# The last projection of a graph network, in seven block products for pairs of row blocks

## The chip, the cores and the metric

The kernel runs on one core of a Trainium2 chip. The metric is the device time of one execution in microseconds. Engines are named as in the profile: PE is TensorE (PEld its weight loads), DVE is VectorE, ACT is ScalarE, POOL is GpSimd, SP is SyncE, which only issues transfers here.

## The reference

Everything is float32: x is [1024, 512], there are 16384 edges, 16 blocks of conditioning [256, 512], and four layers of attention and gated feed-forward between two graph convolutions.

```python
def _gcn(x, src, dst, W, b, n):
    deg = segment_sum(ones_like(src), dst, n)
    dinv = where(deg > 0, deg ** -0.5, 0)
    norm = dinv[src] * dinv[dst]
    h = x @ W
    return segment_sum(h[src] * norm[:, None], dst, n) + b

h0 = relu(layernorm(x))
h = batchnorm(h0);  h = _gcn(h, ..., gcn_in_w, gcn_in_b, n)
for i in range(4):
    h = h + attention(ln(h), cond, Wq[i], Wk[i], Wv[i], Wo[i])
    val, gate = split(ln(h) @ geglu_w[i] + geglu_b[i])
    h = h + (val * gelu(gate)) @ ffo_w[i] + ffo_b[i]
h = _gcn(h, ..., gcn_out_w, gcn_out_b, n)
out = x + h + h0
```

The change is about `x @ W` of the last `_gcn`: [1024, 512] times [512, 512].

## The kernel before, in words

The 1024 rows are eight row blocks of 128 (NB = 8), kept in SBUF as `h[0]` to `h[7]`. A 128x128 block of the edge-count matrix for each pair of row blocks is `counts[d][:, s, :]`; the graph convolution is then a matrix product (`aggregate`, L648 to L659). It takes the projected rows in two parts, high and low (`parts_out`), that are each exact in the twelve-bit format of its matmuls.

Most large products are computed with seven block products instead of eight: a matrix is split into 2 x 2 blocks, sums of blocks are made beforehand (`sums_of_a` and `sums_of_b`, four additions or subtractions each), and the seven products are put together in PSUM and by additions. `multiply` (L301) issues one block product, two matmuls over the two halves of a 256-long sum. `attn_out_pair` (L852 to L883) is an earlier use on two row blocks with two PSUM banks, ab and cd, each of which holds two 256-wide results. `wo_sums` makes the four sums of a weight matrix on GpSimd into the one tile `wos`.

The last stage, before the change:

- In the last layer's last part (r = 3), `load_last` fetches the last weight `w_out` (two transfers on SP's queue) and its bias, and issues the reload of the counts (`ce`) on GpSimd's queue. Also in the last two parts, `base_of` makes `base` = x + h0 for each row block on VectorE.
- `ffn_out` finishes h in two steps, s = 0 (row blocks 0, 1, 4, 5) and s = 1 (2, 3, 6, 7).
- `turn_first` turns the eight row blocks on TensorE (L184) and copies them out of PSUM into `lnT` (tile name ln2T), two copies each on ScalarE (L1106).
- L1315 and L1316: GpSimd adds the bias to the eight `base` tiles.
- `project_block` (L461) computes one row block of the projection with four matmuls of a 512-wide moving tile; `into_parts` scales it into the high part on ScalarE (L1321) and takes the low part on VectorE (L1322).
- L1332: a branch that is taken only when the edges are not sorted by destination; here it is not. L637 has the same one ahead of the first aggregation.
- `aggregate` (L655), and `into_out` (L1327, L1328) per row block: VectorE scales and adds `base`, SP stores.

The order in which instructions stand on each engine's queue is set before the run by the framework's planner: it takes the instructions in the order in which the code traces them as their priority, simulates the engines, and lets a later one go first where an earlier one is not ready in its simulation. A branch splits the program into stretches that are planned one by one. `tc.issue_after` and `waiting_for` force an order by hand; none is used in the last stage. Tiles come from pools of a fixed number of buffers: `psum` eight banks, `work` ten tiles of 128x512 (`t512`), `accs` six of them (`acc_tile`), `slots` 36 of 128x1024.

Of the kernel before, what the change touches and what calls it, by code (L numbers as in the profile page):

```python
# [14 lines left out]
OP = mybir.AluOpType  # L15
AX = mybir.AxisListType

P = 128
# [5 lines left out]
def gnn_kernel(  # L24
# [26 lines left out]
    nc = tc.nc  # L51
# [3 lines left out]
    BS, M, DC = cond.shape  # L55
# [4 lines left out]
    NB = N // P  # L60
# [31 lines left out]
    def bank(name):  # L92
        return psum.tile([P, 512], F32, tag="bank", name=name)

    def t512(name, dtype=F32):
        return work.tile([P, 512], dtype, tag="t512", name=name)
# [4 lines left out]
    def slots_of(n, name):  # L101
        return [slot(f"{name}_{i}") for i in range(n)]

    def load_w(w2d, name):

        w = slots_of(2, name)
        for i in range(2):
            load_w.last = nc.sync.dma_start(
                w[i], w2d[2 * i * P:2 * (i + 1) * P, :].rearrange("(k p) f -> p k f", p=P)
            )  # L110
        return w

    def load_row(vec, offset, name):
        t = rows.tile([P, D], F32, tag="row", name=name)
        nc.sync.dma_start(
            t, bass.AP(tensor=vec.tensor, offset=vec.offset + offset, ap=[[0, P], [1, D]])
        )
        return t

    def four(t):  # L120
        return t.rearrange("p (a b) -> p a b", a=4)
# [58 lines left out]
    def transposed(t, name):  # L180

        pt = bank(f"tr_{name}")
        for k in range(4):
            transposed.last = nc.tensor.transpose(pt[:, k * P:(k + 1) * P],  # L184
                                                  t[:, k * P:(k + 1) * P], ident)
        return pt
# [30 lines left out]
    def sums_of_a(t, a11, a12, a21, a22, s1, s2, s4):  # L217

        t.tensor_tensor(s1, a21, a22, OP.add)
        t.tensor_tensor(a21, a11, a21, OP.subtract)  # L220
        t.tensor_tensor(s2, s1, a11, OP.subtract)
        t.tensor_tensor(s4, a12, s2, OP.subtract)

    def halves_of(t):
        return t.rearrange("p (a b) -> p a b", a=2)
# [70 lines left out]
    def multiply(to, left, right, cols_of, start):  # L296

        for n, (l0, l1, r0, r1) in enumerate(cols_of):
            at = to if len(cols_of) == 1 else to[:, n * (r1 - r0):(n + 1) * (r1 - r0)]
            for k in range(2):  # L300
                nc.tensor.matmul(at, left[:, k, l0:l1], right[:, k, r0:r1],  # L301
                                 start=start and n == 0 and k == 0,
                                 stop=n == len(cols_of) - 1 and k == 1, skip_group_check=True)
# [67 lines left out]
    first = gp.tile([P, 2], F32, name="first")  # L371
# [53 lines left out]
    for nb, xn in enumerate(scaled(xb, mean, root, "x", xb)):  # L425
        with tc.issue_after(cond_turned.ins):
            pt = transposed(xn, f"x{nb}")
        c0 = (nb % 4) * P
# [38 lines left out]
    def project_block(*args):  # L467
        for _ in project_steps(*args):
            pass
# [175 lines left out]
    def of_twelve_bits(rows):  # L645
        return [t.bitcast(F32R) for t in rows]

    def aggregate(parts, name, emit):  # L648

        for ds in [(0, 1), *((d,) for d in range(2, NB))]:  # L650
            pa = [bank(f"agg_{name}_{d}") for d in ds]
            for s in range(NB):
                for d, to in zip(ds, pa):
                    for i, part in enumerate(parts):
                        nc.tensor.matmul(to, counts[d][:, s, :], part[s],  # L655
                                         start=(s == 0 and i == 0),
                                         stop=(s == NB - 1 and i == 1))
            for d, to in zip(ds, pa):
                emit(d, to)  # L659

# [21 lines left out]
    def acc_tile(name):  # L682
        return accs.tile([P, 512], F32, tag="acc", name=name)
# [148 lines left out]
    def wo_sums(wo):  # L832

        b11, b12, b21, b22 = (wo[k][:, :, d * M:(d + 1) * M] for k in range(2) for d in range(2))
        t1, t2, t3, t4 = (halves_of(wos[:, i, :]) for i in range(4))
        for to, of, less in ((t1, b12, b11), (t3, b22, b12), (t2, b22, t1), (t4, b21, t2)):
            nc.gpsimd.tensor_tensor(to, of, less, OP.subtract)
        return [b11, b21, b22, t4, t1, t2, t3]
# [46 lines left out]
    def order7(blk, s1, s2, s4):  # L885

        return [blk[0], blk[1], s4, blk[3], s1, s2, blk[2]]
# [20 lines left out]
    class Quad:  # L908
# [3 lines left out]
        def __init__(self, l, r, c, left, right, fT):  # L912
            self.n, self.c, self.fT = f"{l}_{r}_{c}", c, fT
            self.cv = l * 2 * DFF // P + r * KC + c
            self.left, self.right = left, right

        def product(self, i, to, start):
            multiply(to, self.left[i], self.right[i],
                     [(self.c * P, (self.c + 1) * P, 0, 512)], start)

        def first(self):
            self.a = bank(f"ga_{self.n}")
            self.product(0, self.a, True)
            self.s1 = acc_tile(f"gs1_{self.n}")
            nc.scalar.copy(self.s1, self.a)
# [8 lines left out]
        def rest(self):  # L934
            n, c, bias = self.n, self.c, gcols[:, self.cv:self.cv + 1]
            pb, pc, pd = (bank(f"{x}_{n}") for x in ("gb", "gc", "gd"))
            self.product(5, pb, True)
            u2 = acc_tile(f"gu2_{n}")
            nc.vector.tensor_tensor(u2, pb, self.s1, OP.add)
            self.product(6, pc, True)  # L940
            u3 = acc_tile(f"gu3_{n}")
            nc.vector.tensor_tensor(u3, pc, u2, OP.add)  # L942
            self.product(4, pd, True)
            g1 = t512(f"g1_{n}")
            nc.vector.tensor_tensor(g1, pd, u3, OP.add)  # L945
            self.gate(g1, n)
            self.product(3, pc, False)
            g0 = t512(f"g0_{n}")
            nc.vector.tensor_tensor(g0, pc, u2, OP.add)
            self.gate(g0, n)  # L950
            self.product(2, pd, False)
            v1 = acc_tile(f"gv1_{n}")
            nc.vector.scalar_tensor_tensor(v1, pd, bias, u2, OP.add, OP.add)
            f0, f1 = (self.fT[i][c // 2][:, c % 2, :] for i in range(2))
            nc.vector.tensor_tensor(f1, v1, g1, OP.mult)
            return lambda: nc.vector.scalar_tensor_tensor(f0, self.a, bias, g0, OP.add, OP.mult)
# [140 lines left out]
    def turn_first(l, blocks):  # L1097

        for nb in blocks:
            xn, c0 = xns.pop(nb), nb % 4 * P  # L1100
            if l < L:
                turn(xn, lnT[nb // 4], c0, LN2W + l * KC, LN2B + l * KC, f"ln2_{l}_{nb}")
            else:
                pt = transposed(xn, f"hT_{nb}")
                for k in range(2):
                    nc.scalar.copy(lnT[nb // 4][k][:, :, c0:c0 + P],  # L1106
                                   four(pt)[:, 2 * k:2 * k + 2, :])

    lnT = [slots_of(2, f"ln2T_0_{i}") for i in range(2)]
    aggregate(parts_in, "in", into_h_and_norm)  # L1110
# [12 lines left out]
        return (wk, wv, *load_rest(l))  # L1123

    def load_last():
        w = load_w(gcn_out_w, "w_out")
        bias = load_row(gcn_out_b, 0, "bias_out")
        again = slots_of(NB, "ce")
        for d in range(NB):
            counts[d] = by_sources(again[d].bitcast(F32R))  # L1130
            nc.gpsimd.dma_start(again[d].bitcast(F32R).rearrange("p a b -> p (a b)"), c_dram[d])
        return w, bias
# [8 lines left out]
    for l in range(L):  # L1141
# [40 lines left out]
        right = [ln3T[0][0], ln3T[0][1], ln3T[1][1], ln3S[2], ln3S[0], ln3S[1], ln3T[1][0]]  # L1182
# [73 lines left out]
        lnT = None  # L1256
        base, fetched = [], {}
# [14 lines left out]
        for r in range(R):  # L1272
# [27 lines left out]
            else:  # L1300
                lnT = [slots_of(2, f"ln2T_{l + 1}_{i}") for i in range(2)]
                if last:
                    w_out, bias_out = load_last()
# [8 lines left out]
    ready_first(L, left_to_turn[2:])  # L1312
    turn_first(L, left_to_turn)

    for nb in range(NB):  # L1315
        nc.gpsimd.tensor_tensor(base[nb], base[nb], bias_out, OP.add)  # L1316
    hs_out = [rows_of("hs_high_out"), rows_of("hs_low_out")]
    parts_out = [of_twelve_bits(rows) for rows in hs_out]

    def into_parts(nb, ph):  # L1320
        nc.scalar.mul(parts_out[0][nb], ph, dinv[:, nb:nb + 1])  # L1321
        nc.vector.scalar_tensor_tensor(parts_out[1][nb], ph, dinv[:, nb:nb + 1],  # L1322
                                       hs_out[0][nb], OP.mult, OP.subtract)

    def into_out(d, pa):
        ot = t512(f"ot_{d}")
        nc.vector.scalar_tensor_tensor(ot, pa, dinv[:, d:d + 1], base[d], OP.mult, OP.add)  # L1327
        nc.sync.dma_start(out[d * P:(d + 1) * P, :], ot)  # L1328

    for nb in range(NB):  # L1330
        project_block(nb, lnT, w_out, "out", into_parts)
    with tc.If(unsorted > 0):  # L1332
        add_left(slot("left_out"), hs_out, base, dinv, "out")
    aggregate(parts_out, "out", into_out)


# [35 lines left out]
```

## Time and profile before

| | us |
|---|---|
| median of 3 runs | 2534.37 (2533.81 to 2534.73) |
| the profiled execution | 2532.89 |
| its span in the profile | 2531.1 |
| PE busy | 2506.6 (99%) |
| DVE busy | 1403.6 (55%) |
| POOL busy | 646.0 (26%) |
| ACT busy | 557.3 (22%) |
| granted TensorE clock, mean | 1.0 |

Matmul durations overlap, since matmuls are pipelined: the pace is read from the starts of consecutive ones. Each f32 matmul appears as two instructions ("passes" below). A timeline row gives start, duration, engine, line, operation, out<-in tiles and shapes, and in brackets how long the engine had been idle and what released it. A summary of a tile gives minimum/median/maximum duration in ns and the first and last start in us.

### The profile page before, as it was taken

How to read it: one execution, taken by the hardware profiler on the slowest of the kernel's cores; microseconds unless marked ns; L12 is line 12 of the kernel's file. 1: busy time of each engine (PE TensorE's matmuls, PEld its weight loads, DVE VectorE, ACT ScalarE, POOL GpSimd, SP SyncE). 2: the span in 40 equal slices, each digit the busy share in tenths (PEclk: the TensorE clock that was granted, in tenths of full speed). 3: DMA queues.
4: the chain of work that ended last, by engine and by line, in shares of the span. 5: the costliest groups of instructions: out<-in, count | busy, mean ns of one | idle time of the engine just before them, and what ended most of it. 6: DMA issues, size and time to landing. Idle time of an engine off the chain costs nothing. (4 is left out here: it accounts for less than half of the span.)

```text
span 2531.1 us, 32228 instructions
## 1 busy us (share of the span) xinstructions
PE 2506.6 (99%) x12464; PEld 1768.6 (70%) x12464; DVE 1403.6 (55%) x3026; ACT 557.3 (22%) x1318; POOL 646.0 (26%) x539
## 2 busy tenths in 40 slices
PE   8999999999999999999999999999999999999999
PEld 5778886666578887655587888556676888566565
DVE  9655566544574556544474556644484455654551
ACT  7322222111122223111122222111112222211111
POOL 0322224532210003533320003253320002352410
PEclk9999999999999999999999999999999999999999
DMA  5302232111122112010211212110112121111020
GB/s 179 131 31 91 92 128 64 38 50 35 61 64 70 46 59 76 26 54 17 96 38 67 72 63 67 34 55 17 59 67 64 53 78 60 44 34 64 11 88 34
DMA packets 67136, 156.81 MB, mean 62 GB/s; under 512 B 5576, under 2 KB 5904, under 8 KB 66976
## 3 DMA queue, kind: packets, MB, share of 16 engines
q1 hardware_dynamic: 64880, 149.25, 17.8%
q0 software_dynamic: 1376, 4.30, 0.5%
q8 instruction: 103, 1.69, 0.3%
q10 hardware_dynamic: 720, 1.11, 0.1%
q14 instruction: 57, 0.47, 0.1%
HBM read 133.66 MB, written 20.97 MB: 61 GB/s over the span
## 5 line engine op out<-in xcount | busy, mean ns | idle before, releaser
L301 PE MATMUL ga<-ln3T,wval 128*128 128x512 f32 x512 | 233.9, 593 | 0.0
L932 ACT ACTIVATE g<-g,gcols 128x512 f32<-128x512 f32 x128 | 92.4, 722 | 430.9 <-DVE g L945 366.3
L301 PEld LDWEIGHTS ga<-ln3T,wval 128*128 128x128 f32 x512 | 96.0, 190 | 109.9 <-issue 109.0
L776 ACT ACTIVATE pr<-sc,nmax 128x256 f32<-128x256 f32 x256 | 118.0, 473 | 176.8 <-DVE nmax L771 176.8
L847 POOL TENSOR_TENSOR os<-oT 128x256 f32<-128x256 f32 x12 | 8.7, 726 | 566.9 <-DVE oT L822 566.9
L1006 POOL TENSOR_TENSOR hall<-fu,hall 128x512 f32<-128x512 f32 x24 | 30.4, 1269 | 429.0 <-DVE fu L1005 429.0
L301 PE MATMUL pa_v<-wv,ct 128*128 128x256 f32 x512 | 123.1, 379 | 0.0
L301 PE MATMUL fa<-wff,fT 128*128 128x256 f32 x512 | 121.6, 379 | 0.0
L301 PE MATMUL gc<-ln3S,wgate 128*128 128x512 f32 x256 | 120.4, 593 | 1.1 <-DVE gu L942 1.1
L301 PE MATMUL pc_v<-wv,ct 128*128 128x256 f32 x512 | 121.0, 379 | 0.0
L301 PE MATMUL pd_v<-wvs,ct 128*128 128x256 f32 x512 | 121.0, 379 | 0.0
L301 PE MATMUL pd_k<-ct,wks 128*128 128x256 f32 x512 | 121.0, 379 | 0.0
L301 PE MATMUL pc_k<-ct,wk 128*128 128x256 f32 x512 | 120.9, 379 | 0.0
L301 PE MATMUL gd<-ln3T,ges 128*128 128x512 f32 x256 | 120.6, 593 | 0.0
L301 PE MATMUL gb<-ln3S,ges 128*128 128x512 f32 x256 | 120.3, 592 | 0.0
L301 PE MATMUL gc<-ln3T,wgate 128*128 128x512 f32 x256 | 120.3, 592 | 0.0
L301 PE MATMUL gd<-ln3S,ges 128*128 128x512 f32 x256 | 120.3, 592 | 0.0
L301 PE MATMUL pa_k<-ct,wk 128*128 128x256 f32 x480 | 116.2, 385 | 0.0
L301 PEld LDWEIGHTS fa<-wff,fT 128*128 128x128 f32 x512 | 97.3, 190 | 21.7 <-issue 9.6
L301 PEld LDWEIGHTS pd_k<-ct,wks 128*128 128x128 f32 x512 | 97.3, 190 | 13.2
L301 PEld LDWEIGHTS pd_v<-wvs,ct 128*128 128x128 f32 x512 | 97.3, 190 | 13.2
L301 PEld LDWEIGHTS pc_k<-ct,wk 128*128 128x128 f32 x512 | 97.3, 190 | 13.2
(318 smaller groups left out, 4883.5 us busy)
## 6 DMA issues: line engine op xcount, KB each, us to landing
ct<-cond_dram SPq DMA_DIRECT2D x72, 512.0 KB, 4.5
wval<-in_L_gnn_geglu_w_dram SPq DMA_DIRECT2D x32, 512.0 KB, 3.6
wgate<-in_L_gnn_geglu_w_dram SPq DMA_DIRECT2D x32, 512.0 KB, 4.6
wff<-in_L_gnn_ffo_w_dram SPq DMA_DIRECT2D x32, 512.0 KB, 4.6
cond_dram<-ct SPq DMA_DIRECT2D x24, 512.0 KB, 3.2
cond<-in_L_gnn_cond_dram SPq DMA_DIRECT2D x32, 256.0 KB, 4.4
ct<-cond_dram SPq DMA_DIRECT2D x24, 256.0 KB, 4.5
wk<-in_L_gnn_Wk_dram SPq DMA_DIRECT2D x8, 512.0 KB, 5.3
```

Source lines behind the costliest of these rows:

```text
L301: nc.tensor.matmul(at, left[:, k, l0:l1], right[:, k, r0:r1], start=start and n == 0 and k == 0, stop=n == len(cols_of) - 1 and k == 1, sk ...
L776: nc.scalar.activation(pr3[:, a, :], ps3[:, a, :], AF.Exp, bias=nmax[:, a:a + 1], accum_out=tot[:, a:a + 1])
L847: t.tensor_tensor(s1, a21, a22, OP.add)
L932: nc.scalar.activation(pre, pre, AF.Gelu, bias=gcols[:, cg:cg + 1])
L1006: t.tensor_tensor(h21, halves_of(u2), h21, OP.add)
```

## The change

The last projection is computed for pairs of row blocks (c, c + 4), c = 0 to 3, with seven block products per pair in the manner of `attn_out_pair`. The pairs are worked through two at a time, (0, 1) and then (2, 3); within two pairs, the steps alternate between them. `wo_sums` makes the weight's sums on GpSimd in `load_last`; each pair's sums of the turned rows (`sum_left`) are made on VectorE for c = 0 and on GpSimd for the others. The projected rows are gathered in SBUF tiles (`rows`) and go from there into `into_parts`. Of the two copies of each turned block, one is now on VectorE. The eight bias additions are traced behind the projection, and the last aggregation takes its sources in the order 4, 5, 0, 1, 6, 7, 2, 3.

```diff
-    def aggregate(parts, name, emit):
+    def aggregate(parts, name, emit, order=range(NB)):
 ...
-            for s in range(NB):
+            for n, s in enumerate(order):
                 for d, to in zip(ds, pa):
                     for i, part in enumerate(parts):
                         nc.tensor.matmul(to, counts[d][:, s, :], part[s],
-                                         start=(s == 0 and i == 0),
-                                         stop=(s == NB - 1 and i == 1))
+                                         start=(n == 0 and i == 0),
+                                         stop=(n == NB - 1 and i == 1))
 ...
                 for k in range(2):
-                    nc.scalar.copy(lnT[nb // 4][k][:, :, c0:c0 + P],
-                                   four(pt)[:, 2 * k:2 * k + 2, :])
+                    copy = nc.vector.tensor_copy if k else nc.scalar.copy
+                    copy(lnT[nb // 4][k][:, :, c0:c0 + P], four(pt)[:, 2 * k:2 * k + 2, :])
 ...
     def load_last():
-        w = load_w(gcn_out_w, "w_out")
+        w = wo_sums(load_w(gcn_out_w, "w_out"))
 ...
-    for nb in range(NB):
-        nc.gpsimd.tensor_tensor(base[nb], base[nb], bias_out, OP.add)
 ...
+    class OutPair:
+        def __init__(self, c, right):
+            self.c, self.right = c, right
+            self.left = [lnT[i][k][:, :, c * P:(c + 1) * P] for i in range(2) for k in range(2)]
+            self.ab, self.cd = bank(f"hw_ab_{c}"), bank(f"hw_cd_{c}")
+            self.s1, self.u = acc_tile(f"hw_s_{c}"), acc_tile(f"hw_u_{c}")
+            self.rows = [t512(f"hw_{c}_{i}") for i in range(2)]
+
+        def product(self, i, to, start):
+            multiply(to, self.left[i], self.right[i], [(0, P, 0, M)], start)
+
+        def first(self):
+            a = self.ab[:, :M]
+            self.product(0, a, True)
+            nc.scalar.copy(self.s1[:, :M], a)
+            self.product(1, a, False)
+            nc.scalar.copy(self.rows[0][:, :M], a)
+
+        def sum_left(self, t):
+            more = acc_tile(f"hw_t_{self.c}")
+            s1, s2, s4 = (x.rearrange("p (a b) -> p a b", a=2)
+                          for x in (more[:, :M], more[:, M:], self.s1[:, M:]))
+            sums_of_a(t, *self.left, s1, s2, s4)
+            self.left = order7(self.left, s1, s2, s4)
+
+        def rest(self):
+            (b, c, d), (u2, u3) = (self.ab[:, M:], self.cd[:, :M], self.cd[:, M:]), (
+                self.u[:, :M], self.u[:, M:])
+            add = nc.vector.tensor_tensor
+            self.product(5, b, False)
+            add(u2, b, self.s1[:, :M], OP.add)
+            yield
+            self.product(6, c, True)
+            add(u3, c, u2, OP.add)
+            yield
+            self.product(4, d, False)
+            add(self.rows[1][:, M:], d, u3, OP.add)
+            yield
+            self.product(3, c, False)
+            add(self.rows[1][:, :M], c, u2, OP.add)
+            into_parts(self.c + 4, self.rows[1])
+            yield
+            self.product(2, d, False)
+            add(self.rows[0][:, M:], d, u2, OP.add)
+            into_parts(self.c, self.rows[0])
+            yield
 ...
+    for c in (0, 2):
+        pairs = [OutPair(c + i, w_out) for i in range(2)]
+        for pair in pairs:
+            pair.first()
+        for pair in pairs:
+            pair.sum_left(nc.gpsimd if pair.c else nc.vector)
+        for _ in zip(*(pair.rest() for pair in pairs)):
+            pass
     for nb in range(NB):
-        project_block(nb, lnT, w_out, "out", into_parts)
+        nc.gpsimd.tensor_tensor(base[nb], base[nb], bias_out, OP.add)
     with tc.If(unsorted > 0):
         add_left(slot("left_out"), hs_out, base, dinv, "out")
-    aggregate(parts_out, "out", into_out)
+    aggregate(parts_out, "out", into_out, [4, 5, 0, 1, 6, 7, 2, 3])
```

## The prediction

> **What bounds the kernel now.** I read the page's first part, the waits of TensorE, the timeline of each engine from 2330 us to the end, and then one earlier stage that already computes what the change introduces. First the page's busy times and, from the list of waits after 130 us, every wait of the matmul queue:
>
> ```profile
> PE 2506.6 (99%) x12464; PEld 1768.6 (70%) x12464; DVE 1403.6 (55%) x3026; ACT 557.3 (22%) x1318; POOL 646.0 (26%) x539
> ...
> PE fd L301 <- DVE fs L978: 1.9, 1, 1.9
> PE agg_out L655 <- DVEq L1332: 1.7, 1, 1.7
> PE gc L301 <- DVE gu L942: 1.1, 1, 1.1
> ```
>
> TensorE is the bound: 2506.6 of 2531.1 us, and after the head it waits only three times, 4.7 us together. So the change is worth the matmul passes it takes away, less the waits it creates. The stage it touches, by the timelines of TensorE, ScalarE and VectorE (start, duration, engine, what; a merged row holds several instructions), with one row of the chain that ended last:
>
> ```profile
> 2465.02 3.66 PE L184 MATMUL tr_hT<-ident,hall 128*128 128x128 f32 x32
> 2468.51 27.63 PE L461 MATMUL hw_out<-w_out,ln2T 128*128 128x512 f32 x64
> 2497.81 0.47 PE L655 MATMUL agg_out<-hs_high_out,ce 128*128 128x512 f32 x1 [1.67 <-DVEq L1332]
> ...
> 2497.81 29.29 PE agg_out L655 x128
> ...
> 2465.66 4.52 ACT L1106 COPY ln2T<-tr_hT 128x256 f32<-128x256 f32 x16 [8.48 <-PE tr_hT L184]
> 2496.18 0.69 ACT L1321 ACTIVATE hs_high_out<-hw_out,dinv 128x512 fp32r<-128x512 f32 x1 [2.75 <-PE hw_out L461]
> ...
> 2496.90 0.75 DVE L1322 SCALAR_TENSOR_TENSOR hs_low_out<-hw_out,dinv,hs_high_out 128x512 fp32r<-128x512 f32 x1 [2.68 <-ACT hs_high_out L1321]
> ```
>
> The 32 matmuls of the projection are 64 passes (f32 counts double here), paced (27.63 - 0.59)/63 = 0.429 us apart: 27.47 us, ending at 2495.98. Then ScalarE scales the last block, VectorE takes the remainder until 2497.65, and only 0.16 us later TensorE starts the aggregation, although its first matmul needs block 0, ready for 25 us. The releaser is VectorE's queue at the branch of L1332. The first branch, L637, looks the same from the other side (VectorE, whose input was ready, waited for TensorE's queue there):
>
> ```profile
> 85.17 0.17 DVE L134 TENSOR_SCALAR v_deg<-deg 128x8 f32<-128x8 f32 x1 [4.13 <-PEq L637]
> ```
>
> So I take the branch for a meeting point of the engines. The stage from the first projection pass to the first aggregation pass is 2497.81 - 2468.51 = 29.30 us, and everything after it is 29.29 us of aggregation (128 passes, 0.229 us each) plus one output block: unchanged work that shifts as a whole.
>
> **The passes.** The edit replaces 32 products with a 512-wide moving tile by 4 pairs x 7 products x 2 = 56 with a 256-wide one, 112 passes. Their pace is in an earlier stage of this kernel, attn_out_pair, which has the same products and two half banks each (TensorE, ScalarE, VectorE):
>
> ```profile
> 2135.94 1.03 PE L301 MATMUL wab<-wo,oT 128*128 128x256 f32 x4
> 2136.80 1.03 PE L301 MATMUL wcd<-wos,oT 128*128 128x256 f32 x4
> 2137.66 1.03 PE L301 MATMUL wab<-wos,os 128*128 128x256 f32 x4
> 2138.53 1.03 PE L301 MATMUL wcd<-wos,os 128*128 128x256 f32 x4
> 2139.39 1.03 PE L301 MATMUL wab<-wo,oT 128*128 128x256 f32 x4
> 2140.25 1.03 PE L301 MATMUL wcd<-wos,oT 128*128 128x256 f32 x4
> 2141.12 1.03 PE L301 MATMUL pa_v<-wv,ct 128*128 128x256 f32 x4
> 2141.98 1.03 PE L301 MATMUL wcd<-wo,om 128*128 128x256 f32 x4
> ...
> 2137.00 0.37 ACT L867 COPY om<-wab 128x256 f32<-128x256 f32 x1 [3.73 <-PE wab L301]
> 2137.86 0.37 ACT L869 COPY ou<-wcd 128x256 f32<-128x256 f32 x1 [0.49 <-PE wcd L301]
> ...
> 2141.32 0.42 DVE L879 TENSOR_TENSOR hall<-wcd,hall 128x256 f32<-128x256 f32 x1 [0.44 <-PE wcd L301]
> ```
>
> One product is (2141.98 - 2135.94)/7 = 0.863 us. 28 products: 24.16 us. Saved on passes: 27.47 - 24.16 = **3.31 us**.
>
> **The handoffs.** Two blocks of one pair share a bank, so a product waits until the reader of the other half has finished. The rows show it: the code has the product for d (wcd<-wos,os) ahead of the one for b (wab<-wos,os), but b ran first, while ScalarE read c out of the same bank (2137.86 to 2138.23); and a foreign product, pa_v, was put ahead of the last wcd, which had to follow the addition at 2141.32. So the planner fills such places with whatever is ready. One handoff costs 0.20 us from the end of a product to the reader's start (2141.12 to 2141.32), 0.42 us of addition (0.37 of copy) and an estimated 0.05 to 0.1 us back: about 0.7 us, against the 0.863 us in which the other pair's product runs, since the change alternates two pairs product by product. Spare: 0.15 us. Inside the first two pairs I find each handoff covered; between the first two and the last two, ScalarE has the s1 copies of the new pairs beside two scalings of 0.69 us, and I take 0.6 us of stall. Bounds: 0 (the planner moves the later pairs' first products into any hole) and 14 us: five handoffs in each of four pairs (two around the first two products, three in the second bank), 20 x 0.7, if nothing alternates.
>
> **The inputs.** Splitting the 16 copies between ScalarE and VectorE can't start the projection sooner: it starts at 2468.51, when the transposes end, and does not wait for a copy now. The copies finish about 1.5 us sooner (2470.18 now), limited by the transposes' pace of 0.44 us a block. Then the left sums: four per pair, POOL's at the duration of the like row in pair_sums, the weight sums at that of wo_sums (instruction summaries of two tiles: minimum/median/maximum ns):
>
> ```profile
> L847 POOL TENSOR_TENSOR os<-oT x12: 719/727/732, 226.6 to 2122.8; 128x256 f32<-128x256 f32 x12
> ...
> L837 POOL TENSOR_TENSOR wos<-wo,wos x8: 1260/1266/1268, 148.1 to 1889.7; 128x512 f32<-128x512 f32 x8
> ...
> L108 SPq DMA_DIRECT2D w_out<-in_L_gnn_gcn_out_w_dram x2: 386/402/419, 2406.3 to 2406.7; - x2
> DMA to landing us min/median/max: 3.6/4.5/5.3
> ```
>
> Pair 1's blocks are copied by about 2467.3, so its four sums (2.9 us) are done by 2470.3; its first use, after four opening products and pair 0's, is at 2472.8. Pairs 2 and 3 need 5.8 us of POOL with some ten to spare. Cost: 0; if that cover is gone, 0.7 us for each sum.
>
> The weight sums (4 x 1.27 = 5.1 us) can start at 2406.7 + 5.3 = 2412 and are needed at 2472. On POOL they stand ahead of these (POOL's timeline, then the summaries of the tiles ce and base):
>
> ```profile
> 2432.12 4.28 POOL L1131 DMA_DIRECT2D ce<-c_dram  x8
> ...
> DMA to landing us min/median/max: 3.6/7.4/10.0
> ...
> L1316 POOL TENSOR_TENSOR base<-base,bias_out x8: 1262/1582/1714, 2330.8 to 2439.6; 128x512 f32<-128x512 f32 x8
> ```
>
> The ce loads (landing 10 us after issue at most) may slip by 5 us and are needed at 2496: free. The bias additions, though last in the code before too, run wherever POOL is idle and their base is there; so tracing them behind the projection leaves them at about these times. They cost nothing, and their move gains nothing.
>
> What POOL can cost is VectorE's time. VectorE and POOL beside each other in the stage that has the other two waits:
>
> ```profile
> 2354.63 0.69 DVE L977 TENSOR_TENSOR fs<-fT,fT 128x512 f32<-128x512 f32 x1
> 2356.91 2.83 DVE L979 TENSOR_TENSOR fs<-fT,fs 128x512 f32<-128x512 f32 x1
> ...
> 2356.40 2.79 POOL L219 TENSOR_TENSOR ges<-wgate,wgate 128x1024 f32<-128x1024 f32 x1
> ...
> 2420.51 0.69 DVE L939 TENSOR_TENSOR gu<-gb,gs 128x512 f32<-128x512 f32 x1 [1.78 <-PE gb L301]
> 2361.19 1.99 PE L301 MATMUL gc<-ln3S,wgate 128*128 128x512 f32 x4 [1.05 <-DVE gu L942]
> 2372.39 1.56 PE L301 MATMUL fd<-wffs,fs 128*128 128x256 f32 x6 [1.89 <-DVE fs L978]
> ```
>
> The addition of two SBUF tiles went from 0.69 to 2.83 us, just as long as POOL's beside it; TensorE's 1.1 and 1.9 us waits end there, at 2361.19 and 2372.39. The weight sums are 5.1 us of such work at 2412 to 2417, after which VectorE had 1.78 us to spare before 2420.51 and so can catch up: I take 0, with 1.9 us as the upper end. [...]
>
> **The end of the stage.** Now one block ends 1.83 us ahead of the aggregation. After: the last product, 0.20, an addition 0.42, a scaling 0.69, a remainder 0.75, the restart 0.16: 2.22 us at least. Two pairs end 0.86 us apart, so VectorE has two additions and three remainders to finish in its last 2.5 us; queued one by one they put the restart 2.65 us after the last product. Cost 0.82 us. The new source order of the aggregation matters only if TensorE doesn't wait at the branch.
>
> **Sum.** 24.16 + 0.6 + 2.65 = 27.4 us against 29.30: 1.9 us less. The profiled execution took 2532.89 us (span 2531.1 and 1.8 around it), 1.5 below the median of the runs; the shift applied to the median gives 2534.37 - 1.9 = **2532.5 us**.
>
> **Rivals.** (A) The branch does not hold TensorE: with sources 4, 5, 0, 1 first, 16 aggregation passes cover the end. 24.8 against 29.3: 4.5 us less, 2529.9. Against it are the two rows at L1332 and L637. (B) Slower: VectorE's queue holds up the handoffs. Between the last two steps of each two pairs it has 2 x 0.42 + 2 x 0.75 = 2.34 us of work for 1.73 us of products, and the four remainders there stretch when POOL sums the next pairs. Break-even is at 1.9/20 = 0.1 us a handoff; eight handoffs late by one remainder's overhang (0.6 us) cost 4.8, less the 0.6 already counted: net +2.3, 2536.7. For it: only 0.15 us of spare; against: the remainders come behind the additions that TensorE waits for. (C) The pairs don't alternate: 20 x 0.7 on top, 24.16 + 14 + 2.2 = 40.4: 11 us slower, 2545.4. The filling of pa_v speaks against it. (D) The bias additions do move behind the pairs' sums: 8 x 1.27 = 10.2 us of POOL from about 2483, ending when the last product does; they stretch the remainders of the end by up to 1.8 us. Net 0, 2534.4.
>
> **Numbers.** Forecast 0.62, A 0.06, B 0.18, C 0.05, D 0.09. A measurement here can tell about 0.2%, 5.1 us. Faster by more needs A and no stall at all, or something unseen: 0.04. Slower by more: C and the far end of B: 0.09. The rest, 0.87, lies within. The range takes the forecast with its bounds on the stalls, B, D and A at its own value: 2529.9 to 2537.0.
>
> **What would show it.** Right: 112 projection passes at L301 0.216 us apart starting near 2468.5; the first aggregation pass near 2495.9 with VectorE's queue at the branch as releaser; the bias additions between 2330 and 2441. A: an aggregation pass before the last remainder ends. B: TensorE waits for VectorE additions in the second half of each two pairs. C: two products of one pair back to back with 0.7 us gaps. Wrong altogether: TensorE waits before 2465 that were not there, or a span that moved by over 5 us.

## The result and the profile after: 4.9 us slower, the loss ahead of the changed stage

The changed kernel takes 2538.65 us (median of 20 runs, 2536.46 to 2541.14), the kernel before, beside it on the same chip, 2533.77 (2532.41 to 2535.42): a ratio of 1.0018, 95% interval 1.0011 to 1.0024. The forecast was 2532.5, within 2529.9 to 2537.0. The profiled execution of the changed kernel took 2538.94 us, with a span of 2537.2, 6.1 more than before.

The page's busy times and, from the list of waits, TensorE's after the head (tile and line <- what it waited for: us in total, times, the longest):

```profile
PE 2508.6 (99%) x12512; PEld 1778.7 (70%) x12512; DVE 1422.4 (56%) x3058; ACT 559.5 (22%) x1318; POOL 661.4 (26%) x555
...
PE gc L301 <- DVE gu L942: 4.2, 2, 3.1
PE agg_out L655 <- PEq L1387: 2.7, 1, 2.7
PE fd L301 <- DVE fs L978: 1.9, 1, 1.9
PE hw_ab L301 <- POOL hw_t L221: 0.6, 1, 0.6
PE hw_ab L301 <- ACT hw_s L1334: 0.3, 1, 0.3
```

TensorE has 48 passes more and is busy for 2 us more, not less. Of before's three waits, fd's is the same, the one ahead of the aggregation went from 1.7 to 2.7, and gc has got a second wait of 3.1 us. That one is in the gated feed-forward part, some 35 us ahead of the new projection. Timelines of TensorE, VectorE and GpSimd there:

```profile
2440.76 3.53 PE L301 MATMUL gc<-ln3S,wgate 128*128 128x512 f32 x4 [3.11 <-DVE gu L942]
2444.09 2.07 PE L301 MATMUL gd<-ln3T,ges 128*128 128x512 f32 x4
2445.99 1.88 PE L301 MATMUL ga<-ln3T,wval 128*128 128x512 f32 x4
...
2432.88 1.64 DVE L978 TENSOR_TENSOR fs<-fs,fT 128x512 f32<-128x512 f32 x1
2434.44 4.87 DVE L979 TENSOR_TENSOR fs<-fT,fs 128x512 f32<-128x512 f32 x1
2439.24 0.68 DVE L939 TENSOR_TENSOR gu<-gb,gs 128x512 f32<-128x512 f32 x1
2440.02 0.69 DVE L942 TENSOR_TENSOR gu<-gc,gu 128x512 f32<-128x512 f32 x1
...
2435.03 1.28 POOL L837 TENSOR_TENSOR wos<-w_out 128x512 f32<-128x512 f32 x1
2436.27 1.27 POOL L837 TENSOR_TENSOR wos<-w_out,w_out 128x512 f32<-128x512 f32 x1
2437.49 1.26 POOL L837 TENSOR_TENSOR wos<-w_out,wos 128x512 f32<-128x512 f32 x1
2438.70 0.57 POOL L1131 DMA_DIRECT2D ce<-c_dram  x1
2439.28 1.28 POOL L837 TENSOR_TENSOR wos<-w_out,wos 128x512 f32<-128x512 f32 x1
```

The weight sums of GpSimd start at 2435.03, not at 2412. VectorE's addition of L979 begins 0.6 us ahead of them and ends at 2439.31, 0.56 us after the third of them: 4.87 us. The same instruction took 0.68 in the kernel before:

```profile
2432.65 0.68 DVE L979 TENSOR_TENSOR fs<-fT,fs 128x512 f32<-128x512 f32 x1
```

Behind it in VectorE's queue stand L939 and L942, which TensorE waits for. And then a second price: the four passes after the wait take 3.33 us from start to start (2440.76 to 2444.09), where four at full speed take 1.72 (four times the 0.429 of the old projection), and with the four behind them it is 5.23 us (to 2445.99) against 3.43. Here is the granted clock, in the table of stretches (stretch: us, TensorE busy, granted clock, DMA share, GB/s):

```profile
2430.00:2436.00 6.00, 6.00 (x15) 1.00 0.12 27
2441.00:2444.00 3.00, 3.00 (x4) 0.51 0.91 262
2447.00:2450.00 3.00, 3.00 (x14) 1.00 0.80 294
```

It is at half for a few microseconds. The same thing stands behind the 1.9 us wait of fd, which both kernels have (TensorE, the changed kernel):

```profile
2372.49 2.68 PE L301 MATMUL fd<-wffs,fs 128*128 128x256 f32 x6 [1.89 <-DVE fs L978]
2374.97 2.50 PE L301 MATMUL fb<-wffs,fs 128*128 128x256 f32 x8
```

Six passes in 1.56 us before, in 2.68 here. That one is no deed of the change (below). The changed stage itself (TensorE, then VectorE at its end):

```profile
2475.38 3.62 PE L301 MATMUL hw_ab<-w_out,ln2T 128*128 128x256 f32 x16
...
2487.47 1.89 PE L301 MATMUL hw_ab<-w_out,ln2T 128*128 128x256 f32 x8
2489.64 1.99 PE L301 MATMUL hw_ab<-w_out,ln2T 128*128 128x256 f32 x8 [0.28 <-ACT hw_s L1334]
2491.47 1.03 PE L301 MATMUL hw_ab<-wos,hw_t 128*128 128x256 f32 x4
2493.15 1.13 PE L301 MATMUL hw_ab<-wos,hw_t 128*128 128x256 f32 x4 [0.65 <-POOL hw_t L221]
...
2495.84 1.89 PE L301 MATMUL hw_cd<-wos,hw_t 128*128 128x256 f32 x8
2497.57 1.89 PE L301 MATMUL hw_cd<-wos,ln2T 128*128 128x256 f32 x8
2499.29 1.89 PE L301 MATMUL hw_cd<-w_out,hw_s 128*128 128x256 f32 x8
2503.90 0.47 PE L655 MATMUL agg_out<-hs_high_out,ce 128*128 128x512 f32 x1 [2.71 <-PEq L1387]
...
2502.77 0.75 DVE L1369 SCALAR_TENSOR_TENSOR hs_low_out<-hw,dinv,hs_high_out 128x512 fp32r<-128x512 f32 x1 [0.19 <-ACT hs_high_out L1368]
```

Eight passes are 1.73 us (2495.84 to 2497.57). The products take from 2475.38 to 2499.29 + 1.73 = 2501.02: 25.64 us. The aggregation goes on 2.88 us later. The stage has 28.52 us against 29.30: 0.78 less. The aggregation behind it takes as long as before (its row of the chain that ended last, beside 29.29):

```profile
2503.90 29.32 PE agg_out L655 x128
```

The stage starts 6.87 us later than before (2475.38 against 2468.51), of which 3.1 are the wait of gc, 1.8 the half clock after it and 1.7 the half clock after fd; 0.3 are spread. 6.87 - 0.78 is the 6.1 of the spans. Without the half clock after fd, which the change didn't bring, it would be 4.4, near the 4.9 of the medians.

### The profile page after: what moved, and what is told of

The parts are those of the page before. It is cut to its first block, busy times and chain, and to the rows that moved or that the text cites. A ratio compares the mean times of both kernels' runs of the same rounds, so it can differ in the third digit from the quotient of the medians.

```text
span 2537.2 us, 32399 instructions
## 1 busy us (share of the span) xinstructions
PE 2508.6 (99%) x12512; PEld 1778.7 (70%) x12512; DVE 1422.4 (56%) x3058; ACT 559.5 (22%) x1318; POOL 661.4 (26%) x555
```

## Experiments

Medians with the runs' range; the ratio is to the kernel before, run beside it, with its 95% interval. My theory was that the weight sums on GpSimd cost the whole loss, by holding up the VectorE addition beside them, and that the stage itself gains about what it should; the rival, that the stage's end or the products ate the gain.

**Sums held back, and sums alone.** The first kernel is the changed one with GpSimd's weight sums waiting for the last addition of the feed-forward part; the second is the kernel before with those sums added and their result unused.

```diff
+        with waiting_for(geglu.last, mybir.EngineType.Pool):
             w = wo_sums(w)
```

```diff
         w = load_w(gcn_out_w, "w_out")
+        wo_sums(w)
```

> The changed kernel, with the four weight sums held on GpSimd until VectorE has made the last sums of the last gated part (a real wait on that addition). Theory 1 (overlap): the loss comes from the weight sums running at 2435 to 2440.6 beside VectorE's sum of L979, which took 4.87 us, so that TensorE waited 3.1 us and then ran 3.4 us at half clock. Then the 3.1 us wait is gone, the stage of the projection keeps its 28.5 us against 29.3, and the time is about 0.8 us below the kernel before: 2532.3 to 2533.8. Theory 2 (handoffs): the loss comes from the projection's own waits; then the time stays at 2537 to 2539.

> The kernel before, with the four weight sums of the last weight added in load_last as the change has them; nothing reads them. Theory 1 (overlap): the sums alone bring the 3.1 us wait before the last gated product and, in part of the runs, 1.7 us for half clock behind it: 3 to 5 us slower than before, 2536.8 to 2538.8. Theory 2 (handoffs): no change, 2533.8 within 0.8.

Sums alone: 2538.74 us (2537.09 to 2541.3), 1.0021 [1.0012, 1.0031]: 5.4 us slower with the old projection. Sums held back: 2534.88 (2533.16 to 2536.18), 1.0005 [0.9996, 1.0014]: 3.8 us under the changed kernel, or 3.3 when each is taken against the kernel before beside it. TensorE, the kernel with the sums alone; its row of the list of waits; then the same row with the sums held back:

```profile
2439.69 3.14 PE L301 MATMUL gc<-ln3S,wgate 128*128 128x512 f32 x4 [3.12 <-DVE gu L942]
```

```profile
PE gc L301 <- DVE gu L942: 4.2, 2, 3.1
```

```profile
PE gc L301 <- DVE gu L942: 1.1, 1, 1.1
```

Both runs show it: the loss is that of the four sums at their place. But the held-back kernel did not fall below the kernel before. Its aggregation, from the chain that ended last:

```profile
2497.51 30.77 PE agg_out L655 x128
```

128 passes took 29.29 before. The granted clock of this kernel from 2498 to 2501 us:

```profile
2498.00:2501.00 3.00, 3.00 (x9) 0.56 0.00 0
```

Half clock behind the wait at the branch eats 1.5 us, more than the stage's gain. So the wait at the branch became the question.

**The branch taken out,** from the held-back kernel and from the kernel before. Both leave out the correction for unsorted edges, which is not entered here.

```diff
-    with tc.If(unsorted > 0):
-        add_left(slot("left_out"), hs_out, base, dinv, "out")
```

> As e1_sums_late, and the branch between projection and aggregation is left out, with the correction for unsorted edges in it (not taken here). If the branch is what holds TensorE until the last remainder, aggregation passes of sources 4, 5, 0, 1 start right behind the last product: 2.5 to 2.9 us less than e1_sums_late. If it is the data (the remainders themselves), no difference to e1_sums_late beyond 0.4 us of the branch itself.

> The kernel before (one row block after the other), without the branch and the correction for unsorted edges in it. Measured against e3_no_branch this is what the seven products are worth where nothing waits at the branch. Theory: the aggregation starts right behind the last product, 1.7 us earlier than in the kernel before: 2531.0 to 2532.5; and e3_no_branch (2529.7) stays 1.0 to 2.2 us below it, the 27.47 us of passes against 25.6 us. Rival: the branch was the whole of e3's gain; then this one comes out at e3's 2529.7 within 0.5.

2529.73 us (2528.84 to 2532.16), 0.9986 [0.9977, 0.9995], and 2531.75 (2530.66 to 2533.04), 0.9992 [0.9983, 1.0001]. Without a branch TensorE goes straight on in both (neither list of waits has one ahead of the aggregation), and the difference, 2.0 us in the medians, is the products' own: 27.47 us against 25.64 in the first kernel's timeline (from 2471.55 to 1.73 after the last product's start at 2495.46), 1.8 us. The branch costs the new stage 5.2 us in the medians and the old one 1.7. The 5.2 are more than the 2.5 to 2.9 expected, because the half clock goes with the wait: 2.8 and 1.5 in the held-back kernel's trace.

**The left sums' tile from another pool** (held-back kernel). The third and fourth pair's sums start late because their tile comes from the six of `accs`.

```diff
-            more = acc_tile(f"hw_t_{self.c}")
+            more = t512(f"hw_t_{self.c}")
```

> As e1_sums_late, with the tile of a pair's first sums (hw_t) taken from the work pool (ten buffers) and not from accs (six), where it had to follow hw_s of the same pairs, which waits for the last product of the pairs before. If that wait is what delays the later pairs' sums on GpSimd (start at 2486.9 after TensorE), they start some 2 to 3 us sooner, the wait of 0.65 us and the 0.8 us hole beside it go: 0.7 to 1.5 us less than e1_sums_late in the profile's stage. If the planner's order or ScalarE is what holds that place, the stage stays at 28.5 us within 0.3.

2534.05 us (2532.19 to 2535.98), 1.0002 [0.9993, 1.0011]. The sums start earlier, but a wait of 0.6 us on ScalarE takes the place of the one on GpSimd; the products take 25.38 us instead of 25.63. As the second expectation had it, the stage up to the aggregation stays: 28.53 us (2470.43 to 2498.96) against 28.56. Half clock behind fd (2.82 us for its six passes) and behind the branch (30.91 us of aggregation) here, too.

**Scaling and remainder in halves** (held-back kernel): each 256-wide half of a projected block is scaled as soon as it is there, which ends VectorE's work sooner.

```diff
-    def into_parts(nb, ph):
+    def into_parts(nb, ph, j):
+        to = slice(j * M, (j + 1) * M)
...
             add(u3, c, u2, OP.add)
+            into_parts(self.c, self.rows[0], 0)
...
             add(self.rows[1][:, M:], d, u3, OP.add)
+            into_parts(self.c + 4, self.rows[1], 1)
```

> As e1_sums_late (branch where it was), with the scaling and the remainder made for each 256-wide half as soon as it is there. Theory: the wait at the branch goes from 2.8 to about 1.9 us, and half clock behind it becomes rarer: 0.9 to 2.0 us below e1_sums_late, 2532.9 to 2534.0. Rival: twice as many instructions on ScalarE and VectorE hold up the handoffs between products; then TensorE waits for VectorE inside the two groups and the time is not below e1_sums_late.

2533.23 us (2531.4 to 2534.91), 0.9998 [0.9989, 1.0007]. VectorE's last remainder, then TensorE's first aggregation pass:

```profile
2494.87 0.48 DVE L1374 SCALAR_TENSOR_TENSOR hs_low_out<-hw,dinv,hs_high_out 128x256 fp32r<-128x256 f32 x1 [0.18 <-ACT hs_high_out L1373]
```

```profile
2496.56 0.47 PE L655 MATMUL agg_out<-hs_high_out,ce 128*128 128x512 f32 x1 [2.72 <-PEq L1392]
```

The time came out within the expectation, but not for its reason: the wait stayed at 2.7 us, and the products took 25.01 us instead of 25.63. The miss that changed my mind: VectorE had ended at 2495.35, and TensorE still stood for another 1.2 us. It doesn't wait for VectorE there.

**VectorE made later, in the kernel before:** two extra multiplications by one on the last low part, ahead of the branch.

```diff
+    for _ in range(2):
+        nc.vector.tensor_scalar(parts_out[1][-1], parts_out[1][-1], 1.0, None, OP.mult)
     with tc.If(unsorted > 0):
```

> The kernel before, with two more passes of VectorE over the last low part (a factor of 1.0) ahead of the branch, so that TensorE's wait there grows from 1.7 to about 2.9 us, the length it has in the changed kernel. If a wait of this length sets TensorE to half clock for the next 3.4 us (seen in the traces of e1, e4 and e7), the time grows by more than the wait: 1.2 us, and in most runs 1.4 to 1.6 us on top: 2535.8 to 2536.6, and the first eight aggregation passes 0.43 us apart. If half clock comes from something else in those kernels, it grows by 1.2 us only: 2534.6.

2535.3 us (2533.94 to 2536.15), 1.0006 [0.9997, 1.0015]: 1.8 us, between the two expectations. VectorE, then TensorE:

```profile
2499.55 0.89 DVE L1333 TENSOR_SCALAR hs_low_out<-hs_low_out 128x512 fp32r<-128x512 f32 x2
```

```profile
2500.60 0.47 PE L655 MATMUL agg_out<-hs_high_out,ce 128*128 128x512 f32 x1 [2.59 <-DVEq L1334]
```

VectorE ends at 2500.44, TensorE goes on 0.16 us later, as in the kernel before: there the wait is one for VectorE. No half clock followed this 2.6 us wait in the profiled execution.

**A short branch** (the kernel with halves): the body corrects one block of eight. It is not entered, so nothing that is executed is missing; for unsorted edges the correction of seven blocks is left out.

```diff
-        for d in range(NB):
+        for d in range(1 if name == "out" else NB):
```

> As e7_halves, with one eighth of the correction in the branch's body (row block 0 of the unsorted edges alone; not taken here). In e7_halves the last remainder ended 1.2 us before TensorE went on, and two 16 KB instruction transfers lay between the last product and the first aggregation pass. If TensorE is held by loading the instructions behind the branch's long body, the wait falls from 2.7 to about 1.8 us and half clock behind it becomes rarer: 0.9 to 2.0 us below e7_halves. If it is the meeting of the engines itself, the wait stays at 2.7 us.

2529.3 us (2528.56 to 2530.36), 0.9982 [0.9973, 0.9991], 3.9 under the kernel with halves. TensorE, then VectorE's last remainder:

```profile
2492.16 1.89 PE L301 MATMUL hw_cd<-w_out,hw_s 128*128 128x256 f32 x8
2494.20 0.47 PE L655 MATMUL agg_out<-hs_high_out,ce 128*128 128x512 f32 x1
...
2495.09 0.49 DVE L1374 SCALAR_TENSOR_TENSOR hs_low_out<-hw,dinv,hs_high_out 128x256 fp32r<-128x256 f32 x1 [0.18 <-ACT hs_high_out L1373]
```

The aggregation starts 0.3 us after the last product and 1.4 us ahead of the end of the last remainder. So this branch is no meeting point of the engines. The gain is more than the expected 0.9 to 2.0 us, since nothing of the wait is left. But this edit changed two things. The first aggregation product carries a wait for VectorE in the kernel before, the changed one and the one with halves, as it takes a PSUM bank that the branch's body uses; with the short body it carries none. TensorE's semaphore instructions at the start of the aggregation (count: minimum/median/maximum ns, first and last start), the kernel before and the changed one:

```profile
L655 PEldq EVENT_SEMAPHORE  x2: 51/734/1418, 2496.3 to 2497.8; - x2
...
L655 PEldq EVENT_SEMAPHORE  x2: 51/51/51, 2503.8 to 2503.9; - x2
```

In the kernel before TensorE stands 1.42 us in this wait; in the changed one it is over by the time TensorE comes to it.

**The whole body in one PSUM bank** (kernel with halves) takes away that wait and keeps the length. The second kernel adds the sums of every second pair on VectorE.

```diff
+        pl = bank(f"left_{name}")
         for d in range(NB):
             nc.sync.dma_start(left.rearrange("p a b -> p (a b)"), left_dram[d])
-            pl = bank(f"left_{name}_{d}")
```

```diff
-            pair.sum_left(nc.gpsimd if pair.c else nc.vector)
+            pair.sum_left(nc.gpsimd if pair.c % 2 else nc.vector)
```

> The changed kernel with the weight sums held until GeGLU is done and the scaling and remainder in 256-wide halves, as in the run with halves, and the correction's body whole, but with one PSUM bank for all its products, so that the first aggregation product no longer waits for VectorE over a bank that it shares with the body. Theory 1 (TensorE is held by that wait on VectorE): TensorE goes on about 0.3 us behind the last product of the projection, as with the short body, and the time is about 2529.3 us. Theory 2 (TensorE is held by loading the instructions that lie behind the long body): the wait ahead of the aggregation stays near 2.7 us and the time near 2533.2 us (2531.6 where the half clock stays away).

> The same with every second pair's weight sums on VectorE instead of GpSimd. By theory 1 there is no wait ahead of the aggregation, the passes of the projection lose their 0.5 to 0.6 us of waits on GpSimd, and the time is 2528.8 us. By theory 2 it is 0.3 to 0.5 us under the kernel with one bank, 2531 to 2533 us.

2532.7 us (2531.14 to 2534.03), 0.9998 [0.9989, 1.0007], and 2533.92 (2532.55 to 2534.83), 1.0001 [0.9992, 1.001]. TensorE with the whole body in one bank:

```profile
2492.48 1.89 PE L301 MATMUL hw_cd<-w_out,hw_s 128*128 128x256 f32 x8
2497.21 0.47 PE L655 MATMUL agg_out<-hs_high_out,ce 128*128 128x512 f32 x1 [2.84 <-PEq L1392]
```

Without any wait for VectorE (its trace has no such semaphore instruction at the start of the aggregation), TensorE stands for 2.84 us. What differs from the short body, where it stood for nothing, is the length of the body that is jumped over. The trace has the branch itself as an instruction of each engine's queue. TensorE's (PEldq) in this kernel, with the short body, in the changed kernel and in the kernel before:

```profile
L1392 PEldq COMPARE_BRANCH  x1: 3765/3765/3765, 2493.3 to 2493.3; - x1
...
L1392 PEldq COMPARE_BRANCH  x1: 344/344/344, 2492.9 to 2492.9; - x1
...
L1387 PEldq COMPARE_BRANCH  x1: 3425/3425/3425, 2500.1 to 2500.1; - x1
...
L1332 PEldq COMPARE_BRANCH  x1: 3365/3365/3365, 2488.3 to 2488.3; - x1
```

Over the long body TensorE's branch takes 3.4 to 3.8 us in every kernel that has it at this place, over the short one 0.34. The other engines' branches take 0.045 to 0.063 us, each at its own time. The kernel before pays the 3.4 us too, but its queue comes to the branch at 2488.3, 7.7 us ahead of the last product's end, and the matmuls that are already queued cover it. In the changed kernel it comes there at 2500.1, 0.9 us ahead of that end, and 2.5 us stay uncovered.

An instruction transfer of 16 KB starts 1.0 to 1.2 us into each of these long branches (at 2494.33 in the kernel with one bank, at 2489.3 in the kernel before); with the short body the next one starts at 2494.04, after the branch has ended. What takes the time inside the branch is not shown: measured are 3765 ns over the long body and 344 over the short. That the transfer is TensorE's is inferred from its time, since the profile does not say whose it is.

The second kernel missed its 2531 to 2533 us: the inner wait shrank by 0.1 us only (0.5 on ScalarE), and half clock followed the 2.7 us wait (30.89 us of aggregation).

**The branch behind the aggregation** keeps the correction whole: it is added to the finished output tiles, and they are stored again when it is taken. Three kernels: the held-back one with this; this with halves and the other pool; this with halves and every second pair's sums on VectorE.

```diff
-    with tc.If(unsorted > 0):
-        add_left(slot("left_out"), hs_out, base, dinv, "out")
...
     aggregate(parts_out, "out", into_out, [4, 5, 0, 1, 6, 7, 2, 3])
+    with tc.If(unsorted > 0):
+        add_left(slot("left_out"), hs_out, ots, dinv, "out")
+        for d in range(NB):
+            nc.sync.dma_start(out[d * P:(d + 1) * P, :], ots[d])
```

> As e1_sums_late, with the branch moved behind the aggregation, where its correction would be added to the output tiles and stored again. Theory: TensorE has no wait between projection and aggregation, so neither the 2.8 us nor the half clock behind it come: 2529.7 to 2531.0, at e3_no_branch's time or up to 1 us above it, for the branch at the end. Rival: the branch costs the same wherever it stands; then 2533.5 to 2535.0.

> All together: weight sums late, hw_t from the work pool, scaling by halves, the branch behind the aggregation. Theory: projection in 24.2 to 25.2 us and no wait behind it, 3.5 to 5.0 us below the kernel before: 2528.5 to 2530.0. Rival: with the aggregation already right behind the last product, the halves only add work, and it comes out at e6_branch_last's time or above.

> The best so far (e6_branch_last: weight sums late, branch behind the aggregation) with scaling by halves as in e7_halves, and the sums of pair 2 on VectorE, so that GpSimd makes one pair's sums at a time and pair 3's are there in time. Theory: the 0.64 us wait for GpSimd in the second two pairs goes, the stage from the first product to the first aggregation pass takes 24.3 to 24.8 us, and the time is 0.5 to 1.2 us below e6_branch_last: 2529.8 to 2530.6, below the kernel before by 0.10 to 0.15%. Rival: VectorE's sums come behind its remainders of the first two pairs and beside GpSimd's, so TensorE waits for VectorE there instead; then the stage stays at 25 us or above.

2531.0 us (2529.59 to 2532.74), 0.9989 [0.998, 0.9998]; 2534.0 (2533.47 to 2536.22), 1.0004 [0.9995, 1.0013]; 2530.38 (2528.82 to 2531.78), 0.9987 [0.9978, 0.9996]. The first takes 3.9 us off the held-back kernel and beats both kernels. The second lost that again, by its own wait in the projection:

```profile
PE hw_ab L301 <- DVE hw_t L221: 2.5, 1, 2.5
```

VectorE, in the same kernel:

```profile
2472.84 0.97 DVE L1374 SCALAR_TENSOR_TENSOR hs_low_out<-hw,dinv,hs_high_out 128x256 fp32r<-128x256 f32 x1 [2.71 <-ACT hs_high_out L1373]
```

One of the remainders, which now come earlier, stands ahead of the first pair's left sums in VectorE's queue, and there VectorE waits 2.7 us for ScalarE. The left sums start 4.6 us after the first product instead of 0.9, and then take 0.83 to 0.95 us each beside GpSimd's, which start earlier. The third has no wait above 0.5 us in a stage of 24.72 us (2468.77 to 2493.49 in its timeline). It is the best version that keeps the whole correction: 3.1 us under the kernel before.

## Why the prediction was wrong

**The weight sums' cost of zero failed, in place and in price.** "Can start at 2412" took the landing of the weight for the start. They stand in GpSimd's queue among the ce loads and behind a bias addition, which waits for its base:

```profile
2432.39 1.58 POOL L1386 TENSOR_TENSOR base<-base,bias_out 128x512 f32<-128x512 f32 x1 [13.79 <-DVE base L1270]
```

So they start 23 us later, beside the one VectorE instruction of that part that TensorE is about to need. The prediction had the effect (2.83 us beside one 2.79 us operation) but took one such stretch as the most: it said 1.9 us, the length of fd's wait, as the upper end. Here one addition ended only behind three sums, 4.87 us, and 4.88 in the kernel with the sums alone. How long such an addition is held up differs: here it lasted through three sums; in the kernel before, ahead of that wait of fd and beside four GpSimd sums of the same size from 2366.72 on (1.59 to 1.71 us each), three VectorE additions took 1.64, 1.09 and 1.75 us. What decides is not shown. Measured: 3.1 us of wait and 1.8 of half clock, 5.4 us in the median of the sums alone.

**The half clock was no term of the sum.** Each of the prediction's waits was priced at its own length. Seven of the ten waits of 2.5 to 3.1 us in the 15 traces were followed by half clock, which cost 1.5 to 1.8 us more, and this took the held-back kernel's whole gain.

**The handoffs' 0.6 us were 1.48.** 25.64 - 24.16; most of it is two gaps at the third and fourth pair: 0.44 us ahead of 2489.64, released by ScalarE, and 0.82 ahead of 2493.15, from a tile of six that comes free late. None of them came from the additions between products, which the prediction feared.

**The end's 2.65 us was near (2.88), its reason half right.** VectorE's part ended at 2503.52, 2.50 us after the last product, and with the 0.16 us of the kernel before that alone gives 2.66: the count of VectorE's work was good. But the branch was read as a meeting point, from two rows. In the old stage TensorE stood in the wait for VectorE that its first aggregation product carries. At L637 TensorE's own branch took 3.62 us, from 81.3 to 84.9, just ahead of the row that was read; why VectorE waited for it there was not tried. In the new stage TensorE stood in its branch, from 2500.1 to 2503.5, and that has no term in the sum. With the same long body, shortening VectorE's work left the wait at 2.7, and with a short one it was gone. Rival A, given 0.06, had the mechanism: a branch that doesn't hold TensorE is worth 3.9 us in the kernel with halves. In the changed kernel two things held TensorE until about 2503.5, the branch and the wait for VectorE, so either one alone would have kept nearly all of the 2.88 us.

**Right** were the passes' pace (0.216 us), the alternation of pairs (C did not occur), the bias additions, whose summary shows them where they were, and the copies without effect:

```profile
L1386 POOL TENSOR_TENSOR base<-base,bias_out x8: 1262/1582/1710, 2330.9 to 2446.3; 128x512 f32<-128x512 f32 x8
```

Rival B's net loss of 2.3 was near half the true one, but from another place and mechanism.

**Open.** Why TensorE's queue comes to the branch 7.7 us ahead of its last product's end in the old stage and 0.9 us in the new one. In the new stage each late product follows an addition of VectorE, which may keep the queue back; no run tried it.

## What to carry to other kernels

Before work is added to an idle GpSimd, look at which VectorE instruction it will stand beside and who waits for that one; price it at up to the unbroken run of GpSimd operations (here the addition of 0.68 us took 4.87, until 0.56 us after the third of four sums), and if need be hold it back to a stretch where nobody waits. The branch over the long body took TensorE 3.4 to 3.8 us here, over the short one 0.34, though the body is never entered; that was hidden where TensorE's queue came to it 7.7 us ahead of its matmuls' end, and 2.5 us of it were not where it came 0.9 us ahead. Put such a branch where nothing follows that is urgent: behind the aggregation the kernel took 2531.0 us, ahead of it 2534.88. Price a TensorE wait of about 2 us or more at up to 1.8 us above its length: here half clock followed 12 of 25 waits of 1.9 to 3.1 us and cost 1.5 to 1.8 us.

## What the hardware showed unasked

- In the changed kernel the granted clock falls to half for 3.413 us at a time, on one grid: the trace's clock records begin such stretches at 96.32, 2383.25 and 2451.52 us on their own axis, 670.0 and 20.0 times 3.413 us apart (that axis starts 10.47 us ahead of the timelines' zero).
- Where a wait fell on that grid made the difference in these traces. Adding up TensorE's idle time in each window of the grid, by the starts and ends of its passes, in all 15 traces and behind 130 us: the twelve stretches at half clock each follow a window that was idle for 0.553 of its length or more, and none of the other 10509 windows was idle for more than 0.547. So fd's wait of 1.9 us, the same in every kernel, brought it in 5 of 15 profiled executions, those where it lay wholly in one window; waits of 2.5 to 3.1 us brought it in 7 of 10. The 2.84 us of the kernel with one bank fell 0.45 and 0.38 into two windows, the 2.59 us of the longer wait 0.30 and 0.46, and brought none. Waits of 1.7 us and 1.1 us brought none.
- The jump over the long body left TensorE standing for 2.7 to 3.0 us in six kernels of the new stage (the changed one, held back, other pool, halves, and the two with one bank), with or without a wait for VectorE, and over the short body for nothing.
